# Masked graph attention on one core: two loads of W_v's blocks issued behind the opening products of the last q pair

## The chip, the cores and the metric

The kernel runs on one core of a Trainium2 chip, in float32. The metric is the device time of one execution in microseconds, as the median of repeated runs. Positions in the text, such as 366.93, are microseconds from the start of the span of the profiled execution.

## The reference

One layer of graph attention over 2708 nodes with 1024 features, with a sparse 0/1 matrix adj (about 0.15% ones, some four neighbours a node):

```python
h = relu(layernorm(x))
q = h @ W_q.T + b_q;  k = h @ W_k.T + b_k;  v = h @ W_v.T + b_v
z = (q @ k.T) / sqrt(1024) * adj
attn = softmax(where(z == 0, -10000, z), axis=1)
out = x + relu(attn @ v)
```

## The kernel before, in words

**What is computed instead.** The scores need q and k only where adj has a one, so the kernel doesn't form k: it builds M = W_q^T W_k / 32 at the start, computes q = h M (for all rows but the last 148), and takes the dot product of a row of q with the gathered rows of h of its neighbours. The weighted sum is taken over rows of h too (u = attn h), and W_v is applied last: o = u W_v. Rows are sorted by their number of neighbours, so that a tile of 128 rows needs few gathers.

**Stages on TensorE.** First the products that make M (up to about 104 us), then ten *q pairs* (`q_pairs`, two tiles of 128 rows each, units 0 to 9), then ten *o pairs* (`o_pairs`, units 10 to 19) and a lone tile. Every unit is a 256 x 1024 by 1024 x 1024 product in Strassen's form with seven products: `multiply` (L1046) and, for the first two, `opened` (L1015). The operands from the rows are a11, a12, a22 and s1 to s4; the weights are the blocks of M (M[:, 0, 0] and so on) and four differences T[:, 0] to T[:, 3], which live in the buffer that traces call wlow. One product is four matmuls of 128x512 in the source and eight in the trace (two passes each). The two opening products of unit n+1 (a11 by M[:, 0, 0] and s1 by T[:, 0], or by M[:, 0, 1] in an o unit) are issued inside unit n by `between` (L1031), ahead of unit n's last product, a22 by T[:, 3].

**The change of weights.** Between the last q pair (unit 9, `last_q`, tiles 18 and 19) and the first o pair M has to turn into W_v while both are in use. W_v's four blocks are loaded by `of_wv`: B22 into T[:, 0] (from where ACT copies it to M[:, 1, 1] and DVE subtracts to form T[:, 1]), B11 into M[:, 0, 0], B21 into M[:, 1, 0]; B12 less B11 is formed earlier in M[:, 0, 1]. The function `after(i)` (L1249) is called between the products of a unit; the loads of B22 and B11 are issued at `after(0)` of unit 9, B21 at `after(3)`. The place T[:, 0] is free when the second opening product of unit 9 has read it, the place M[:, 0, 0] when the first has.

**Queues.** Loads and stores of plain shape are issued by SP (its hardware queue is q1 in the profile), some stores by ACT (q10), and gathers by POOL (the software queue q0). SP and POOL issue in program order, and an instruction that waits holds up all behind it. The results of a q pair are stored to q_late by `store` inside `q_results` (L1086): tile ta after its right half, tile tb after ACT has copied the left half (`c21`, L1101). POOL fetches a tile's q back as `pq` (L833) when its scores are due; for tile 17 that is soon after its store.

**DVE** runs in an order written out by hand (`manual_schedule`): its share of gathered rows (L863 for the scores, L923 for the sums) is cut into pieces by `advance` and put between the additions of the products. One of those, L1093 (`c22`), reads the PSUM bank Y (psy) and makes the right half of the second tile; in the last q pairs it reads Y directly, so the product a22 by T[:, 3], which adds onto the same bank, must come after it:

```python
    def c22(Y, p5):
        behind.append(nc.vector.tensor_add(qb[:, hi], copied(Y) if EARLY <= ta < EARLY + 4 else Y, p5))
```

Of the kernel before, what the change touches and what calls it, by code (L numbers as in the profile page):

```python
# [65 lines left out]
def tile_preln_masked_attention(  # L66
# [12 lines left out]
    nc = tc.nc  # L79
# [120 lines left out]
    M = core.tile([P, 2, 2, 4, NB], FT, name="M")  # L200
# [108 lines left out]
    def follow(steps):  # L309

        for step in steps.split():
            first, *only = step[1:].split(".")
            first, *last = first.split("-")
            first = int(first or 0)
            if step[0] == "s":
                stats(range(first, int(last[0] if last else first) + 1))
            elif step[0] == "m":
                moments(first)
            elif step[0] == "r":
                root(first)  # L320
            elif step[0] == "a":
                apply(first, *[range(int(o[0]), int(o[-1]) + 1) for o in only])
            elif step[0] in "hk":
                keep(first, step[0] == "h")
            elif step[0] == "+":
                owe(first)
            elif step[0] == "p":
                counted(first)
            elif step[0] == "c":
                counts(*halves[first])  # L330
            elif step[0] == "o":
                sorted_at.append(sort(*halves[first]))
            elif step[0] == "w":
                pooled.close()
                with tc.issue_after((behind if first < EARLY else products)[-1].ins):
                    entered.append(put(first, int(last[0]) + 1))
            elif step == "z":
                pooled.enter_context(tc.manual_schedule(engines={mybir.EngineType.Pool}))
                with tc.issue_after(entered[-1].ins):
                    reload(EARLY, NT)  # L340
            elif step[0] == "b":
                reload(*halves[first])
            elif step[0] == "g":
                squared(first)
            else:
                if step[0] == "e":
                    counted(first)
                if step[0] != "j":
                    found(first, *[range(int(o[0]), int(o[-1]) + 1) for o in only])
                if step[0] != "i":  # L350
                    listed(first)
# [81 lines left out]
    T = wlow.rearrange("p (k a) (b w) -> p k (a b) w", a=2, b=2)  # L433
# [12 lines left out]
    with tc.tile_pool(name="w", bufs=1, side="left") as wp:  # L446
# [11 lines left out]
        t1 = [work.tile([P, D], FT, tag="hT", name=f"t1_{k}", bufs=2) for k in range(2)]  # L458
# [145 lines left out]
    def small(name):  # L604
        return half.tile([P, NB], FT, tag="half", name=name, bufs=14)
# [402 lines left out]
    def add_block(bank, a, b, last=True):  # L1008
        for c in range(4):
            mm = nc.tensor.matmul(bank, a[:, c, :], b[:, c, :], start=False, stop=(c == 3), skip_group_check=True)  # L1010
        return mm
# [3 lines left out]
    def opened(n):  # L1015

        if n not in banks_of:
            return
        X, Z = banks_of[n]
        ops = ops_of[n][0]  # L1020
        add_block(X, ops["a11"], M[:, 0, 0])
        Y = psum.tile([P, NB], FT, tag="acc", name="psy")
        nc.scalar.copy(Y, X)
        if n == FIRST:
            follow("o0")
        products.append(add_block(Z, ops["s1"], T[:, 0] if units[n][0] == "q" else M[:, 0, 1]))
        p5 = small("p5")
        nc.scalar.copy(p5, Z)
        opened_of[n] = Y, p5

    def between(n):  # L1031

        if n == len(units) - 1:
            single["first"] = one_started(single["banks"], single["turned"][:, 0:4, :])
        else:
            opened(n + 1)

    def one_started(banks, a):

        X, Z = banks  # L1040
        add_block(X, a, M[:, 0, 0])
        first = small("p_single")
        nc.scalar.copy(first, X)
        return first

    def multiply(n, results, after):  # L1046


        X, Z = banks_of.pop(n)
        ops = ops_of.pop(n)[0]  # L1050
        Y, p5 = opened_of.pop(n)
        after(0)
        after(1)
        products.append(add_block(Y, ops["s2"], T[:, 1]))
        u2 = small("u2")
        nc.scalar.copy(u2, Y)
        after(2)
        add_block(X, ops["a12"], M[:, 1, 0])
        results[0](X)
        after(3)  # L1060
        products.append(add_block(Z, ops["s4"], M[:, 1, 1]))
        results[2](Z, u2)
        after(4)
        products.append(add_block(Y, ops["s3"], T[:, 2]))
        results[1](Y, p5)
        after(5)
        between(n)
        add_block(Y, ops["a22"], T[:, 3])
        results[3](Y)
        after(6)  # L1070
# [119 lines left out]
    def of_wv(i, j):  # L1190

        return wv[j][:, i * 4:(i + 1) * 4, :]
# [26 lines left out]
    last_q = len(q_pairs) - 1  # L1219
# [13 lines left out]
    for n, unit in enumerate(units):  # L1233
# [15 lines left out]
        def after(i):  # L1249
# [15 lines left out]
                    with tc.issue_after(sorted_at[-1].ins):  # L1265
                        nc.vector.memset(g, 0.0)
            b11, t1, b21, b22 = M[:, 0, 0], M[:, 0, 1], M[:, 1, 0], M[:, 1, 1]
            for at, place, src in (((-2, 0), t1, of_wv(0, 0)), ((0, 0), T[:, 0], of_wv(1, 1)), ((0, 0), b11, of_wv(0, 0)),
                                   ((0, 3), b21, of_wv(1, 0))):
                if (n - last_q, i) == at:  # L1270
                    nc.sync.dma_start(place, src)
            if (n - last_q, i) == (0, 4):
# [302 lines left out]
```

## Time and profile before

| | |
|---|---|
| median of 3 runs | 630.65 us (630.48 to 630.88) |
| the profiled execution | 635.63 us |
| its span | 633.9 us |
| mean granted TensorE clock | 0.994 |
| HBM read, written | 146.70 MB, 43.36 MB |

The profile is one execution, taken by the hardware profiler. PE is TensorE's matmuls and PEld its weight loads, DVE VectorE, ACT ScalarE, POOL GpSimd, SP the sync engine; SPq or POOLq is an engine's sequencer or queue. A row such as `ps<-M,a` names what an instruction writes and reads, without the buffers' numbers; a bracket at a row's end tells how long the engine stood idle before it and what ended that. The granted clock is a share of TensorE's full clock. A tile has 128 x 1024 float32 values, 0.52 MB; a block of W_v is 128 x 2048, 1.05 MB.

### The profile page before, as it was taken

The page shows a single profiled execution, that of the slowest core. Times are in us where ns is not written, and L with a number is a line of the kernel's source. Part 1 is how long each engine was busy: PE and PEld are TensorE (multiplying, and loading weights), DVE is VectorE, ACT ScalarE, POOL GpSimd, SP SyncE. Part 2 cuts the span into 40 slices and gives each one's busy share as a digit, 9 for nine tenths or more (in the row PEclk, how much of TensorE's full clock was granted, in tenths as well). Part 3 has the DMA queues.
Part 4 walks back from the last instruction along what each step waited for, and adds up shares of the span by engine and source line. Part 5 has one row for each costly group of instructions (what it writes and reads, how often), then busy time and mean ns, then how long its engine had stood idle before and what let it go on. Part 6 is the DMA issues. An engine that isn't in the chain of part 4 may idle for free.

```text
span 633.9 us, 6066 instructions
## 1 busy us (share of the span) xinstructions
PE 623.0 (98%) x1579; PEld 312.0 (49%) x1579; DVE 525.2 (83%) x1022; ACT 291.6 (46%) x421; POOL 370.7 (58%) x394
## 2 busy tenths in 40 slices
PE   9999999999998999999999989999999999999996
PEld 5777766444444544444444434444444444444442
DVE  5999879898897845899897879998988998988741
ACT  3538985749477372443332333444433324342300
POOL 2639960885766677666543432878566776762241
PEclk9999999999999999999999989999999999999999
DMA  8999997598788469996686999899999999996391
GB/s 333 407 365 316 340 351 301 207 320 307 262 257 337 135 196 369 296 410 191 207 343 197 362 346 305 261 335 318 330 285 344 291 297 307 341 286 172 102 295 71
DMA packets 65089, 182.19 MB, mean 287 GB/s; under 512 B 9960, under 2 KB 20024, under 8 KB 64409
## 3 DMA queue, kind: packets, MB, share of 16 engines
q0 software_dynamic: 26656, 86.02, 43.3%
q1 hardware_dynamic: 31594, 71.53, 32.7%
q10 hardware_dynamic: 6798, 24.20, 9.8%
q8 instruction: 14, 0.23, 0.2%
q14 instruction: 27, 0.21, 0.1%
HBM read 146.70 MB, written 43.36 MB: 300 GB/s over the span
## 4 chain that ended last, share of the span: by engine, by line
PE 96%; DMA 3%; issue 0%; POOL 0%; SPq 0%; DVE 0%; ACT 0%; POOLq 0%
PE ps L1010 44%; PE psy L1010 32%; PE ps_y L476 6%; PE ps_x L476 4%; PE ps_z L476 4%; PE pt L415 3%; DMA M<-in_wv_dram 2%; DMA qr<-h_dram,tab 1%; PE ps_y L511 1%; PE ps_h L1226 0%; PE ps_v L594 0%; DVE y_alone L1391 0%; POOL out_dram L1375 0%; ACT q L1101 0%; POOLq L1397 0%
## 5 line engine op out<-in xcount | busy, mean ns | idle before, releaser
L610 POOL DMA_INDIRECT g<-h_dram,tab x93 | 120.5, 1296 | 62.7 <-ACT u L912 21.7
L1010 PE MATMUL ps<-M,a 128*128 128x512 f32 x320 | 145.8, 599 | 2.0 <-DMA M<-in_wv_dram 2.0
L1010 PE MATMUL psy<-wlow,s 128*128 128x512 f32 x320 | 145.1, 596 | 0.0
L863 DVE SCALAR_TENSOR_TENSOR junk<-g,pq 128x1024 uint8<-128x1024 f32 x92 | 112.4, 1221 | 11.8 <-issue 4.9
L1010 PE MATMUL ps<-M,s 128*128 128x512 f32 x240 | 107.9, 592 | 0.0
L1010 PEld LDWEIGHTS ps<-M,a 128*128 128x128 f32 x320 | 60.4, 192 | 75.4 <-issue 71.2
L1010 PEld LDWEIGHTS psy<-wlow,s 128*128 128x128 f32 x320 | 60.6, 192 | 72.9 <-issue 71.9
L923 DVE SCALAR_TENSOR_TENSOR u<-g,coef,u 128x1024 f32<-128x1024 f32 x70 | 89.7, 1281 | 5.5 <-ACT u L912 4.0
L389 DVE FIND_INDEX8 at<-ones,adj 128x8 uint32<-128x685 f32 (+1 forms) x88 | 74.5, 865 | 0.0
L1010 PEld LDWEIGHTS ps<-M,s 128*128 128x128 f32 x240 | 45.5, 190 | 57.2 <-issue 56.5
L1010 PE MATMUL psy<-wlow,a 128*128 128x512 f32 x160 | 71.9, 592 | 0.0
L368 ACT ACTIVATE sized<-adj 128x2708 uint8<-128x2708 f32 (+1 forms) x22 | 54.2, 2465 | 7.9 <-DMA adj<-in_adj_dram 6.6
L1111 POOL DMA_INDIRECT y<-in_x_dram,tab x19 | 34.6, 1821 | 35.6 <-ACT y L1128 24.2
L298 POOL TENSOR_TENSOR hsum<-hsum,x 128x256 f32<-128x256 f32 (+1 forms) x56 | 38.8, 738 | 25.5 <-DVE wlow L444 21.4
L1010 PEld LDWEIGHTS psy<-wlow,a 128*128 128x128 f32 x160 | 30.4, 190 | 38.3 <-issue 37.1
L808 POOL DMA_INDIRECT out_dram<-y,tab x21 | 27.0, 1287 | 19.2 <-issue 13.1
L1010 PE MATMUL ps<-wlow,s 128*128 128x512 f32 x80 | 36.0, 593 | 0.0
L944 ACT COPY v<-u 128x1024 f32<-128x1024 f32 x19 | 19.8, 1044 | 29.1 <-DVE u L923 25.8
L760 ACT COPY ps<-bp_sb 128x512 f32<-128x512 f32 x42 | 24.6, 595 | 10.3 <-DVE y L1146 9.7
L626 POOL DMA_INDIRECT tab_dram<-tab,pos_i x22 | 21.7, 985 | 11.2 <-DVE pos_i L689 5.7
L276 ACT ACTIVATE x<-x,r 128x1024 f32<-128x1024 f32 (+1 forms) x22 | 25.8, 1232 | 5.2 <-POOL r L266 5.2
L912 ACT ACTIVATE u<-g,coef 128x1024 f32<-128x1024 f32 x16 | 18.4, 1149 | 21.3 <-DVE coef L911 13.2
(253 smaller groups left out, 843.4 us busy)
## 6 DMA issues: line engine op xcount, KB each, us to landing
adj<-in_adj_dram SPq DMA_DIRECT2D x21, 1354.0 KB
x<-in_x_dram SPq DMA_DIRECT2D x21, 512.0 KB
h_dram<-x ACTq DMA_DIRECT2D x21, 512.0 KB
u_dram<-v ACTq DMA_DIRECT2D x19, 512.0 KB
or<-u_dram SPq DMA_DIRECT2D x76, 128.0 KB
q_late<-q SPq DMA_DIRECT2D x12, 512.0 KB
pq<-q_late POOLq DMA_DIRECT2D x12, 512.0 KB
M<-in_wv_dram SPq DMA_DIRECT2D x3, 1024.0 KB
```

Of the source, the lines that this page charges most:

```text
L276: nc.scalar.activation(xs[i][:n], xs[i][:n], AF.Relu, bias=r[:n, 4, i:i + 1], scale=r[:n, 3, i:i + 1])
L298: small.append(nc.gpsimd.tensor_add(hsum[:n, cols], hsum[:n, cols], xt[:n, cols]))
L368: nc.scalar.activation(sized[:n], a[:n, :, :PW], AF.Abs, accum_out=total[:n, t:t + 1])
L389: nc.vector.max_index(at[:n, k - first_k, g, :], ones[:n, 0:8], a[:n, g, :])
L476: mm = nc.tensor.matmul(bank, a_tile(o + H * a[0], a[1], i), b(o), start=first and o == 0, stop=(o == H - 1), skip_group_check=True)
L610: return nc.gpsimd.indirect_dma_start(out=dst, out_offset=None, in_=src, in_offset=off, bounds_check=N - 1, oob_is_err=False)
L760: nc.scalar.copy(return_[h], row[:, h * NB:(h + 1) * NB])
L808: to = nc.gpsimd.indirect_dma_start(out=out, out_offset=bass.IndirectOffsetOnAxis(ap=ptab.bitcast(U32)[:n, t, SLOTS:SLOTS + 1], axis=0), i ...
L863: chained(lambda: nc.vector.scalar_tensor_tensor(junk, g_of[t][s], 1.0, tq[t], op0=ALU.mult, op1=ALU.mult, accum_out=zall[:, t, s:s + 1]))
L923: chained(lambda: nc.vector.scalar_tensor_tensor(u, g_of[t][s], coef[:, s:s + 1], u, op0=ALU.mult, op1=ALU.add))
L1010: mm = nc.tensor.matmul(bank, a[:, c, :], b[:, c, :], start=False, stop=(c == 3), skip_group_check=True)
L1111: return nc.gpsimd.indirect_dma_start(out=y[:n], out_offset=None, in_=x, in_offset=off, compute_op=ALU.add)
```

## The change

The two loads leave `after(0)` of unit 9 and are issued in `between`, at the point where unit 8 has issued the opening products of unit 9:

```diff
         else:
             opened(n + 1)
+        if n == last_q - 1:
+            nc.sync.dma_start(T[:, 0], of_wv(1, 1))
+            nc.sync.dma_start(M[:, 0, 0], of_wv(0, 0))
...
-            for at, place, src in (((-2, 0), t1, of_wv(0, 0)), ((0, 0), T[:, 0], of_wv(1, 1)), ((0, 0), b11, of_wv(0, 0)),
-                                   ((0, 3), b21, of_wv(1, 0))):
+            for at, place, src in (((-2, 0), t1, of_wv(0, 0)), ((0, 3), b21, of_wv(1, 0))):
```

Lines below the addition are three numbers higher in the changed kernel as far as the loop of loads, and two behind it (L1086 is L1089, L1093 is L1096, L1271 is L1273).

On SP's queue, around the end of unit 8, before (or_5 and or_4 are rows for the first two o pairs; q_17 is the second result of unit 8; wlow is T[:, 0]):

```order
L700 DMA or_5_2263<-u_dram_66 32x4x256 [waits DMAHW6_49]
L700 DMA or_5_2263<-u_dram_66 32x4x256 [waits DMAHW7_49]
L1086 DMA q_late_65<-q_17_2153 128x1024 [waits DMAHW0_49,DVE_49,Activation_49]
L1271 DMA wlow_170<-in_wv_dram 128x2048 [waits DMAHW2_49,PE_49]
L1271 DMA M_147<-in_wv_dram 128x2048 [waits DMAHW3_49]
L1271 DMA M_147<-in_wv_dram 128x2048 [waits DMAHW4_49,PE_49]
L700 DMA or_4_2370<-u_dram_66 32x4x256 [waits DMAHW5_49,DMASW2_49,Pool_49]
```

and of the change:

```order
L700 DMA or_5_2263<-u_dram_66 32x4x256 [waits DMAHW6_49]
L700 DMA or_5_2263<-u_dram_66 32x4x256 [waits DMAHW7_49]
L1038 DMA wlow_170<-in_wv_dram 128x2048 [waits DMAHW0_49,PE_49]
L1039 DMA M_147<-in_wv_dram 128x2048 [waits DMAHW2_49]
L1089 DMA q_late_65<-q_17_2153 128x1024 [waits DMAHW3_49,DVE_49,Activation_49]
L1273 DMA M_147<-in_wv_dram 128x2048 [waits DMAHW4_49,PE_49]
L700 DMA or_4_2370<-u_dram_66 32x4x256 [waits DMAHW5_49,DMASW2_49,Pool_49]
```

The store of tile 17's q, which waits for ACT and DVE, has moved from ahead of the two loads to behind them; the names DMAHW0 to DMAHW7 are semaphores that transfers take in turn. Nothing else changes places, on any engine.

On POOL's queue, at the fetch of tile 17's q, before (g are gathered rows, the last of six in a row shown; pq_17 and pq_13 are fetched tiles of q):

```order
L610 DMA g1_1426<-h_dram_63,tab_97 128x1024 [waits DMASW6_49,DVE_49]
L610 DMA g3_1428<-h_dram_63,tab_97 128x1024 [waits DMASW7_49,DVE_49]
L833 DMA pq_17_2353<-q_late_65 128x1024 [waits DMAHW0_49,DMASW0_49]
L833 DMA pq_13_2434<-q_late_65 128x1024 [waits DMASW1_49,DVE_49]
L610 DMA wlow_170<-h_dram_63,tab_97 128x1024 [waits DMASW2_49,DMAHW2_49,DVE_49,Activation_49]
```

and of the change:

```order
L610 DMA g1_1426<-h_dram_63,tab_97 128x1024 [waits DMASW6_49,DVE_49]
L610 DMA g3_1428<-h_dram_63,tab_97 128x1024 [waits DMASW7_49,DVE_49]
L833 DMA pq_17_2353<-q_late_65 128x1024 [waits DMAHW3_49,DMASW0_49]
L833 DMA pq_13_2434<-q_late_65 128x1024 [waits DMAHW0_49,DMASW1_49,DVE_49]
L610 DMA wlow_170<-h_dram_63,tab_97 128x1024 [waits DMASW2_49,DMAHW0_49,DVE_49,Activation_49]
```

The rows stand in the same order; the fetch of pq_17 waits for the store of tile 17 under that store's new semaphore.

DVE's rows behind the subtraction that forms T[:, 1], of the change (u_20 is a sum, q_18 and q_19 are the halves of unit 9's results, junk2 and zall take scores of tile 17):

```order
L1284 TENSOR_TENSOR wlow_170<-wlow_170,M_147 128x2048 [waits DMAHW0_49,PE_49]
L923 SCALAR_TENSOR_TENSOR u_20_2321<-g2_1427,coef_2320,u_20_2321 128x1024 [waits DMASW4_49,Activation_49]
L1099 TENSOR_TENSOR q_18_2299<-ps1_2224,u2_2317 128x512 [waits PE_49]
L863 SCALAR_TENSOR_TENSOR junk2_2390,zall_102<-g6_1431,pq_17_2353 128x1024 [waits DMASW0_49]
L863 SCALAR_TENSOR_TENSOR junk2_2392,zall_102<-g7_1432,pq_17_2353 128x1024 [waits DMASW1_49,DVE_49]
L1096 TENSOR_TENSOR q_19_2300<-psy_2280,p5_2286 128x512 [waits PE_49]
```

Before, these six stand in the same order, as L1282, L923, L1096, L863, L863 and L1093; the subtraction waits for DMAHW2 there. Behind the opening products of unit 10 PE's product that adds onto the bank psy_2280 waits for the last of them, before and now.

## The prediction

> **What bounds the kernel now.** I read the page's busy shares first, then who waited for whom on PE, then the chain that ended last, then the timelines of PE, DVE and POOL around the one wait that the change touches. The page, and the two long waits of PE:
>
> ```profile
> PE 623.0 (98%) x1579; PEld 312.0 (49%) x1579; DVE 525.2 (83%) x1022; ACT 291.6 (46%) x421; POOL 370.7 (58%) x394
> PE pt L415 <- DMA qr<-h_dram,tab: 2.1, 1, 2.1
> PE ps L1010 <- DMA M<-in_wv_dram: 2.0, 1, 2.0
> ```
>
> PE is busy 98% of the span, and it waits for data twice. The second wait is for a block of W_v in M, that is B11, needed by the opening product of the first o unit. The chain that ended last, in order of time, shows what made B11 late (start us, us, what):
>
> ```profile
> 351.20 0.59 ACT q L1101
> ...
> 351.81 0.34 SPq L1086
> ...
> 352.25 0.38 SPq L1271
> ...
> 352.95 13.84 DMA M<-in_wv_dram
> ```
>
> SP first waits for ACT to finish tile 17's q (L1101), issues its store (L1086), then the two loads. B11 is issued at 352.95 and takes 13.84 us. The price on PE, from its timeline (start, duration, form, count):
>
> ```profile
> 344.13 3.60 PE L1010 MATMUL ps<-wlow,s 128*128 128x512 f32 x8
> ...
> 361.30 3.60 PE L1010 MATMUL psy<-wlow,s 128*128 128x512 f32 x8
> 366.93 5.37 PE L1010 MATMUL ps<-M,a 128*128 128x512 f32 x8 [2.03 <-DMA M<-in_wv_dram]
> 372.13 3.60 PE L1010 MATMUL ps<-M,s 128*128 128x512 f32 x8
> 375.57 3.60 PE L1010 MATMUL psy<-wlow,a 128*128 128x512 f32 x8
> ```
>
> Products start 3.43 us apart when nothing is late (375.57 - 372.13 is 3.44). The opening product could have started at 361.30 + 3.43 = 364.73 and started at 366.93: 2.20 us. It then took 372.13 - 366.93 = 5.20 us instead of 3.43: another 1.77 us. The second part is the clock. Stretches of the span: columns are PE, PEld, DVE, ACT and POOL busy us, then PE's granted clock, DMA share and GB/s:
>
> ```profile
> 196.00:206.00 10.00, 7.92 (x22) 3.94 (x21) 6.46 (x23) 6.06 (x10) 8.11 (x11) 0.87 0.82 302
> 367.00:372.00 5.00, 5.00 (x8) 2.11 (x9) 2.05 (x3) 0.00 (x0) 3.37 (x3) 0.66 1.03 355
> ```
>
> Right behind the wait the clock was 0.66 over 5 us, that is 1.7 us lost; behind the other wait (2.08 us idle between 196 and 206) it was low as well. So a wait of some 2 us costs nearly 4: 2.20 + 1.77 = 3.97 us is all that the change can take away directly.
>
> **The change: what it removes.** T's B22 place is last read by the product that starts at 344.13 and ends about 347.6; the B11 place is free still earlier. SP has nothing else queued then, so B22 is issued at about 347.7 instead of 352.25 and B11 at 348.4 instead of 352.95, 4.5 us sooner. B11 could take up to 16 us and still be there for 364.73; it took 13.84. Both old waits on these loads (PE's 2.20 + 1.77, and below DVE's 1.71) go. Instruction counts and the order on PE, DVE, ACT and POOL stay as they were, so no work is added.
>
> **What is late next.** Two products behind that opening product PE depends on DVE: the product psy<-wlow,a at 375.57 (a22 times T3 of the last q pair) adds onto the bank Y that DVE has to read first, in the addition that makes tile 19's right half (L1093). DVE's timeline there, then POOL's:
>
> ```profile
> 364.17 2.29 DVE L1282 TENSOR_TENSOR wlow<-wlow,M 128x2048 f32<-128x2048 f32 x1 [1.71 <-DMA wlow<-in_wv_dram]
> ...
> 371.21 1.23 DVE L863 SCALAR_TENSOR_TENSOR junk<-g,pq 128x1024 uint8<-128x1024 f32 x1 [2.95 <-DMA pq<-q_late]
> ...
> 373.63 0.69 DVE L1093 TENSOR_TENSOR q<-psy,p 128x512 f32<-128x512 f32 x1
> ```
>
> ```profile
> 353.99 1.74 POOL L610 DMA_INDIRECT g<-h_dram,tab  x1 [0.53 <-DVE u L929]
> 359.75 1.15 POOL L833 DMA_DIRECT2D pq<-q_late  x2 [4.02 <-DMA q_late<-q]
> ```
>
> DVE stood 2.95 us at 371.21 until tile 17's q (pq) was back on chip, and L1093 is third in line behind that. It ends at 373.63 + 0.69 = 374.32. Today PE comes at 375.57 and notices nothing. With the old wait gone PE comes at 364.73 + 2 x 3.43 = 371.59 and has to wait till about 374.35, if pq lands when it lands now: 2.75 us.
>
> So what counts is by how much pq moves; call it d (negative is sooner). DVE's earlier 1.71 us don't help: they only lengthen its wait for pq. Pq is fetched by POOL, behind its gathers on the software queue q0, and only after the store of tile 17, which stands on SP's queue q1. The DMA queues in 350-356, 356-364 and 364-371 (packets, MB, share of the engines):
>
> ```profile
> DMA packets 461, 1.69 MB, mean 281 GB/s; under 512 B 49, under 2 KB 49, under 8 KB 461
> q0 software_dynamic: 435, 1.58, 82.1%
> ...
> DMA packets 747, 3.43 MB, mean 429 GB/s; under 512 B 86, under 2 KB 86, under 8 KB 571
> q1 hardware_dynamic: 310, 1.86, 55.4%
> q0 software_dynamic: 293, 1.04, 31.9%
> ...
> q1 hardware_dynamic: 365, 1.83, 63.8%
> q0 software_dynamic: 373, 0.88, 37.5%
> ```
>
> and from SP's timeline seven row loads of the next o unit but one:
>
> ```profile
> 358.49 12.76 SPq L700 DMA_DIRECT2D or<-u_dram  x7
> ```
>
> In 350-356 the gathers have the engines nearly alone, at 281 GB/s; once the W_v loads run, everything together moves at 429, but q0 falls from 1.58 MB in 6 us to 1.04 in 8. The moved loads bring this squeeze forward by some 5 us. Two bounds for d. Below: about 5.5 us at 429 instead of 281 GB/s move 0.8 MB more, which at 400 GB/s is 2.0 us; if all of it came to q0, d = -2.0. Above: the store now has both loads (128 x 2048 f32 each, 2.1 MB) ahead of it on q1. At q1's 1.83 MB in 7 us they take 8.0 us, less the 4.1 us by which they are issued sooner than the store is (347.7 against 351.81): the store lands up to 3.9 us later, POOL asks for pq that much later, and if nothing hides it, d = +3.9. What hides it: q0 moved 0.88 MB in 364-371, of which pq is 0.52, so 0.36 MB of older gathers stood ahead of pq even at 364. And the 0.8 MB gained at the front meets seven row loads of 0.13 MB each, 0.92 MB, that stand ready on q1 and take their turns against q0, where today they move mostly after pq. Both bounds are thus nearly used up, and I take **d = -0.2**.
>
> The sum: -3.97 (old wait and its slow clock) + 2.75 - 0.2 = 2.55 (new wait) + 1.77 (its slow clock, since two waits of 2.0 to 2.1 us both had it) = **+0.35 us**. [...]
>
> All this is made on the profiled execution, 635.63 us with a span of 633.9; it lies 0.8% above the median of 630.65. I carry the difference over to the median: 630.65 + 0.35 = **631.0 us**. A difference within 0.2%, 1.26 us, can't be told from none.
>
> **Rivals.**
> *Full gain.* If pq lands by 371.21 - 2.75 = 368.46, PE never waits: 630.65 - 3.97 = 626.7. For it: B11 is surely early, and the profiled execution may be more crowded than the timed ones. Against: d would have to pass its lower bound of -2.0; at that bound 0.75 us of wait remain, 627.4. The gain would last to the end, although the lone tile is tight there:
>
> ```profile
> 609.07 1.25 DVE L705 STREAM_TRANSPOSE T_alone<-or 128x1024 f32<-128x1024 f32 x1 [10.76 <-DMA or<-u_dram]
> 610.78 3.60 PE L1010 MATMUL ps<-M,T_alone 128*128 128x512 f32 x8
> DVE u L1127 <- PE ps L1010: 3.0, 4, 1.2
> DVE p L1123 <- ACT taken L1077: 2.9, 3, 1.6
> ```
>
> T_alone is ready at 610.32, 0.46 us ahead of PE; but DVE, whose sums feed it, waits 5.9 us for PE's results between 460 and 560 alone (the last two rows), so it moves up with PE by the 3.97.
>
> *The new wait without the slow clock.* The wait of 2.55 us is there, but the clock holds: -3.97 + 2.55 = -1.42, 629.2 us, just past the limit of what can be told. Two waits out of two that were slowed speak against it; for it, both of those ended with the clock's drop at once, so how far into a wait the drop is decided can't be read. [...]
>
> *Slower: the store behind the loads.* POOL's request for pq waits for a store that now queues behind both loads. If the gathers ahead of pq are through before it has landed, nothing hides the rest: with half of the 3.9 us showing, d = +2.0, the wait is 4.75 and the sum -3.97 + 4.75 + 1.77 = +2.55, 633.2 us; with all of it +4.45, 635.1. It decides from d = +0.7 (wait 3.46) on: then the time is over 1.26 us longer. For it: only 0.36 MB of gathers were left at 364, less than 2 us of work. Against: they are squeezed sooner now and so last longer.
>
> *No change in what is issued when.* Something else on SP holds the loads until 352: 630.65. The queue shows nothing between the last row load of the unit before and these loads, so this is unlikely.
>
> **How the numbers follow.** The forecast (wait moved, clock halved, d between -1.5 and +0.7) gets 0.52, full or nearly full gain 0.10, the wait without slow clock 0.16, slower 0.20, no change 0.02. With d in these bounds the sum is between -0.95 and +1.25, within the limit but for sizes that are off (0.03 on either side). Of the third case 0.09 is beyond the limit and 0.07 within. Faster: 0.10 + 0.09 + 0.03 = 0.22; slower: 0.20 + 0.03 = 0.23; the same: 0.46 + 0.07 + 0.02 = 0.55. The range goes from 627.4 (d = -2.0, which leaves most of the full gain out) to 633.2 (half of the store's delay showing): some 0.17 stay outside.
>
> **What would show it.** Right: B22 and B11 issued near 347.7 and 348.4; PE's wait for M gone; in its place a wait of 2 to 3 us of a psy product for DVE's q addition, near 371.6, with the clock below 1 behind it; pq at DVE within 1 us of 371.2. Wrong: no wait of PE there (full gain), the clock at 1.00 behind the wait, or a pq later than 371.9. The forecast as a whole fails if PE's products behind the last q pair start over 1.3 us sooner or later than now.

## The result, and the profile after

| | before | after |
|---|---|---|
| median of 6 runs each, side by side | 630.75 us (630.23 to 631.53) | 635.98 us (634.79 to 638.39) |
| ratio to before, 95% interval | | 1.0085 [1.0072, 1.0098] |
| the profiled execution | 635.63 us | 635.39 us |
| its span | 633.9 us | 633.6 us |
| mean granted clock of the profiled execution | 0.994 | 0.992 |

The change costs 5.2 us; the prediction was 631.0 with a range up to 633.2. The two profiled executions are equally long although the medians differ by 5.2 us: the one of before was unusually long for its kernel, 5 us over its median, and one place where that shows is a wait near 200 us (`pt`, 2.1 us, with the clock at 0.50 from 203.42 to 206.84) that the profile of after doesn't have. So positions are compared from one common mark, the start of the second opening product of unit 9 (`ps<-wlow,s`), at 344.13 before and 340.40 after; after's positions are 3.73 us lower by nothing that the change does.

The waits of PE, of after (us in total, times, longest):

```profile
PE psy L1010 <- DVE q L1096: 4.2, 1, 4.2
```

The wait for M, B11, isn't among them any more, and one for DVE's addition out of bank Y has come. SP's queue and PE's timeline, of after:

```profile
344.03 0.35 SPq L1038 DMA_DIRECT2D wlow<-in_wv_dram  x1
344.43 0.43 SPq L1039 DMA_DIRECT2D M<-in_wv_dram  x1
348.08 0.33 SPq L1089 DMA_DIRECT2D q_late<-q  x1
```

```profile
340.40 3.60 PE L1010 MATMUL ps<-wlow,s 128*128 128x512 f32 x8
...
361.00 3.60 PE L1010 MATMUL ps<-M,a 128*128 128x512 f32 x8
364.44 3.60 PE L1010 MATMUL ps<-M,s 128*128 128x512 f32 x8
372.28 6.37 PE L1010 MATMUL psy<-wlow,a 128*128 128x512 f32 x8 [4.25 <-DVE q L1096]
378.48 3.60 PE L1010 MATMUL psy<-wlow,s 128*128 128x512 f32 x8
```

The loads go out 4.5 us sooner than before, as foreseen (344.03 + 3.73 = 347.76). The opening product on B11 starts on time. The product behind the next, a22 by T[:, 3], was due at 364.44 + 3.43 = 367.87 and starts at 372.28: 4.41 us late. The one behind it follows 6.20 us later instead of 3.43, so the slow clock takes 2.77 us more. The chain that ended in this wait, and DVE's timeline:

```profile
347.47 0.59 ACT q L1104
...
348.08 10.76 DMA q_late<-q
...
359.39 0.49 POOL pq L833
...
359.93 10.29 DMA pq<-q_late
...
371.62 0.62 DVE q L1096
```

```profile
369.12 1.23 DVE L863 SCALAR_TENSOR_TENSOR junk<-g,pq 128x1024 uint8<-128x1024 f32 x1 [6.40 <-DMA pq<-q_late]
...
371.54 0.69 DVE L1096 TENSOR_TENSOR q<-psy,p 128x512 f32<-128x512 f32 x1
```

It is the chain that the prediction followed: store of tile 17, fetch, two scores, addition, PE. The row of 10.29 us begins at 359.93, with POOL's second fetch (tile 13's, issued right behind), and ends after DVE's first score of tile 17 has begun. Tile 17's own fetch was issued at 359.36 and landed 9.7 us later; that is what DVE waited for. Pq reaches DVE 369.12 - 340.40 = 28.72 us after the mark, before it was 371.21 - 344.13 = 27.08: the shift d is +1.64 us where -0.2 was taken.

Where d comes from stands in the DMA queues. The prediction's stretches 350-356, 356-364 and 364-371 of before are 346.27-352.27, 352.27-360.27 and 360.27-367.27 of after:

```profile
DMA packets 412, 2.36 MB, mean 394 GB/s; under 512 B 36, under 2 KB 36, under 8 KB 211
...
q1 hardware_dynamic: 217, 1.65, 69.6%
q0 software_dynamic: 195, 0.72, 32.1%
...
DMA packets 712, 3.06 MB, mean 382 GB/s; under 512 B 81, under 2 KB 81, under 8 KB 597
...
q0 software_dynamic: 293, 1.07, 35.6%
...
q0 software_dynamic: 539, 1.45, 66.6%
q1 hardware_dynamic: 532, 0.87, 37.4%
```

The first stretch moves 0.67 MB more than before (2.36 against 1.69), and all of that and more goes to q1: q0, the gathers, fall from 1.58 to 0.72 MB. In the second q0 stays level (1.07 against 1.04), in the third it makes up 0.57 MB (1.45 against 0.88). It is 0.26 MB short where pq should land, at 1.45 MB in 7 us some 1.3 us of work. The third stretch moves 2.33 MB in all against 2.70 before: what the engines gained at the front they lose again at the end, when q1 has less to add (0.87 MB against 1.83). This is the account of one execution; the runs below show that the bytes on q0 alone don't set how late pq is.

### The profile page after: what moved, and what is told of

The parts are those of the page before. It is cut to its first block, busy times and chain, and to the rows that moved or that the text cites. A ratio compares the mean times of both kernels' runs of the same rounds, so it can differ in the third digit from the quotient of the medians.

```text
span 633.6 us, 6066 instructions
## 1 busy us (share of the span) xinstructions
PE 622.3 (98%) x1579; PEld 311.6 (49%) x1579; DVE 524.4 (83%) x1022; ACT 291.5 (46%) x421; POOL 367.0 (58%) x394
## 4 chain that ended last, share of the span: by engine, by line
PE 90%; DMA 5%; DVE 2%; ACT 1%; issue 0%; POOL 0%; POOLq 0%; DVEq 0%; ACTq 0%
PE ps L1010 41%; PE psy L1010 30%; PE ps_y L476 7%; PE ps_x L476 4%; PE ps_z L476 4%; PE pt L415 3%; DMA adj<-in_adj_dram 2%; DMA q_late<-q 2%; DMA pq<-q_late 2%; DVE at L389 1%; PE ps_y L511 1%; PE ps_h L1229 0%; PE ps_v L594 0%; ACT sized L368 0%; DVE junk L863 0%
## 5 line engine op out<-in xcount | busy, mean ns | idle before, releaser
L1010 PE MATMUL ps<-M,a 128*128 128x512 f32 x320 | 144.0, 592 | 0.0
L863 DVE SCALAR_TENSOR_TENSOR junk<-g,pq 128x1024 uint8<-128x1024 f32 x92 | 112.4, 1221 | 14.0 <-DMA pq<-q_late 6.4
L923 DVE SCALAR_TENSOR_TENSOR u<-g,coef,u 128x1024 f32<-128x1024 f32 x70 | 89.7, 1281 | 5.5 <-ACT u L912 4.1
L1010 PE MATMUL psy<-wlow,a 128*128 128x512 f32 x160 | 74.7, 611 | 4.2 <-DVE q L1096 4.2
L476 PE MATMUL ps_y<-wlow 128*128 128x512 f32 x64 | 27.6, 592 | 0.0
```

The lines of the kernel that those rows point to most:

```text
L476: mm = nc.tensor.matmul(bank, a_tile(o + H * a[0], a[1], i), b(o), start=first and o == 0, stop=(o == H - 1), skip_group_check=True)
L863: chained(lambda: nc.vector.scalar_tensor_tensor(junk, g_of[t][s], 1.0, tq[t], op0=ALU.mult, op1=ALU.mult, accum_out=zall[:, t, s:s + 1]))
L923: chained(lambda: nc.vector.scalar_tensor_tensor(u, g_of[t][s], coef[:, s:s + 1], u, op0=ALU.mult, op1=ALU.add))
```

## The experiments

The first four runs were made to tell two theories apart. A: the store of tile 17 waits on q1 behind the two loads, and pq with it. B: the loads take the engines from everything, the gathers on q0 as well as the store. Ratios are to runs of before on the same chip.

### Which queue, which block, or when

**The store on ACT's queue.** The change, with the store of tile 17 issued by ACT (q10, which also carries ACT's stores of u) instead of SP:

```diff
-            (nc.scalar if t < 4 else nc.sync).dma_start(dst, q)
+            (nc.scalar if t < 4 or t == 17 else nc.sync).dma_start(dst, q)
```

> The change, with the store of tile 17's q issued by ACT (queue q10) instead of SP, so that it no longer stands behind the two loads. Theory A (the store behind the loads makes pq late, DVE's addition late, and PE wait at the bank Y): the store lands by 357 instead of 358.8 in that trace's time, pq is then held only by the gathers ahead of it, d falls from +1.6 to between -0.5 and 0, PE's wait for DVE from 4.2 to 2.2-2.7 us with one slow window: 630.5 to 632.5 us, at least 3 us under the change. Theory B (the squeeze: both loads take the engines from the gathers ahead of pq, wherever the store stands): pq is as late as in the change, 635 to 636.5 us.

Measured: 636.56 us against 631.3, ratio 1.0081 [1.0068, 1.0094]. The chain of this kernel:

```profile
347.50 9.91 DMA q_late<-q
...
357.94 11.77 DMA pq<-q_late
```

On a queue with no load ahead the store still takes 9.91 us (10.76 in the change), and pq comes 29.91 us after the mark (369.73 - 339.82), later than in the change. Theory A fell: what stands ahead on SP's queue isn't the point. That the store is late at all still counts for something, since POOL asks for pq only when it has landed.

**Only B11 early.** B22 goes back to its old place (the loop of loads, not shown, has it again):

```diff
         if n == last_q - 1:
-            nc.sync.dma_start(T[:, 0], of_wv(1, 1))
             nc.sync.dma_start(M[:, 0, 0], of_wv(0, 0))
...
```

> Half of the change: B11 issued behind the opening products, B22 left behind the store at its old place. The store has one load ahead of it instead of two. Theory A: the store is about half as late, d between 0 and +0.8, PE's wait for DVE 2.7 to 3.5 us with one slow window: 631 to 633 us, between the two kernels. Theory B: the squeeze starts as early as in the change but with half the bytes: also between, so this run tells A from B only by where the store lands against pq. If B22's later arrival (it is needed for T1 and by ACT for M) costs on its own, it is above 636.

Measured: 631.41 us, ratio 1.0001 [0.9987, 1.0015]. PE's and DVE's rows:

```profile
370.65 5.40 PE L1010 MATMUL psy<-wlow,a 128*128 128x512 f32 x8 [2.87 <-DVE q L1095]
```

```profile
367.49 1.23 DVE L863 SCALAR_TENSOR_TENSOR junk<-g,pq 128x1024 uint8<-128x1024 f32 x1 [3.24 <-DMA pq<-q_late]
```

Here pq comes 27.34 us after the mark (340.15), d = +0.26, and the forecast's picture is what one sees: the wait for B11 is exchanged for one of 2.87 us for bank Y, and the time is the same.

**Only B22 early.** The load of B11 goes back instead.

> Only the load of B22 is issued early, ahead of the store of tile 17; B11 stays behind it. Theory B (the two early loads together squeeze the gathers and the store of tile 17, so pq comes late and PE waits for the addition that reads bank Y): one load ahead of the store squeezes half as long, pq at DVE +0.3 to +1.2 us against before, B11 about as late as before (wait 1.5 to 2.5 us), time 630 to 633. Rival C (it is B22's load, which runs in the gathers' stretch, that does the whole harm, since B11 alone did none): 634 to 637, pq at DVE +1.5 us or later.

Measured: 638.86 us against 634.13, ratio 1.0079 [1.0057, 1.0101], all of the harm with one of the two loads. PE's row there:

```profile
375.60 6.77 PE L1010 MATMUL psy<-wlow,a 128*128 128x512 f32 x8 [3.88 <-DVE q L1095]
```

Theory B had expected less and missed; rival C, that it is B22's load, fitted the time, though pq came 28.35 us after the mark (d = +1.27), a little less late than it had said. The store is nearly on time here (7.97 us); the fetch takes 12.16 us, and PE's wait for B11 is gone here too (its load is issued 8.07 us after the mark, in before 8.82). But B22 also starts later than B11 alone did: it must wait for the second opening product, 3.63 us after the mark (347.72 - 344.09), while B11 alone was issued 0.19 us after it (340.34 - 340.15). So the block and the time had to be parted.

**B11 alone, held back.** A load of 64 KB that waits as B22 does stands ahead of it (shown against B11 alone):

```diff
         if n == last_q - 1:
+            nc.sync.dma_start(T[:, 0, 0, 0:128], of_wv(1, 1)[:, 0, 0:128])
             nc.sync.dma_start(M[:, 0, 0], of_wv(0, 0))
...
```

> Only B11 is issued early, but held back on SP's queue behind a load of 64 KB into a corner of T[:, 0], which must wait until the second opening product has read that place: B11 then starts some 3.5 us later than in the run with B11 alone, where B22 starts in the run with B22 alone, about 4 us ahead of the store. Theory B' (the harm comes from the time at which 1 MB of weights meets the gathers and the store, whichever block it is): the store lands late, pq at DVE +0.8 to +1.8 us, PE waits 3.5 us or more for the addition that reads bank Y, ratio to before 1.005 to 1.010, as with B22 alone (1.0079). Rival C (B22's load or what hangs on it does the harm): ratio 0.998 to 1.003, as with B11 alone (1.0001).

Measured: 635.99 us against 630.95, ratio 1.0067 [1.0047, 1.0088]. In the profiled execution B11 was issued 1.45 us after the mark, not 3.6 (its wait was shorter, as only the corner had to be free), and even that sufficed. The profile was of an execution of 632.75 us, with pq only 0.43 us late; so the kernel was profiled again:

> The kernel with B11 alone, held back, once more for a second profile: the first was of an execution of 632.75 us, while the median of ten was 635.99. Theory B': in an execution near 636 pq is at DVE +0.8 to +2.0 us late and PE waits 3.5 us or more, with one or two windows at half clock behind it. If an execution near 636 has pq no later than +0.5 and PE's wait at 3 us, the loss lies somewhere else and B' doesn't explain the time.

That execution took 640.78 us, longer than any of the ten before (637.19 at most), and PE waited 5.93 us. Its chain:

```profile
351.50 7.58 DMA q_late<-q
...
359.60 14.60 DMA pq<-q_late
```

Rival C fell: issued 1.26 us later, B11's load does nearly the harm of B22's. And this chain has a store of usual length; pq is 3.32 us late (374.22 - 343.82 = 30.40) though POOL asked for it when it always had (15.78 us after the mark, 15.81 in the first profile). It is the fetch that took longer, 14.60 us against 11.68 in the first profile.

What the slower kernels have in common is that q0 moved less in the first 12 us after the mark, when POOL issues the gathers. Of before, of B11 alone, of B11 held back (first and second profile), of B22 alone, and of the change:

```profile
q0 software_dynamic: 862, 2.78, 75.1%
```

```profile
q0 software_dynamic: 857, 2.77, 65.8%
```

```profile
q0 software_dynamic: 759, 2.41, 61.8%
...
q0 software_dynamic: 768, 2.45, 63.5%
```

```profile
q0 software_dynamic: 691, 2.18, 56.7%
```

```profile
q0 software_dynamic: 614, 1.88, 47.9%
```

B11 issued at +0.19 (340.34) goes out ahead of all but the first of the eight gathers that POOL issues from 340.1 to 350.0; q1 moves 1.35 MB in the 12 us instead of 0.38, and q0 loses nothing (2.77 MB): ratio 1.0001. With 0.33 to 0.90 MB lost the ratios are 1.0067, 1.0079 and 1.0085. That orders the kernels, not their executions: with B11 held back q0 lost as much in the first profile as in the second, and pq was 0.43 us late in the one and 3.32 in the other. What makes the difference between these two isn't shown.

### The link through pq and bank Y

**Bank Y copied by ACT**, so that PE needn't wait for DVE's addition, in the change and in before:

```diff
-... copied(Y) if EARLY <= ta < EARLY + 4 else Y, p5))
+... copied(Y) if EARLY <= ta < EARLY + 4 or ta == BARE - 2 else Y, p5))
```

> The change, with the bank Y of the last q pair copied out by ACT (0.59 us) ahead of DVE's addition, as the earlier pairs 8 to 11 do, so that PE's product a22 x T3 waits for ACT and not for DVE. If the bank Y is the only link from the late pq to PE (A and B alike): PE's wait of 4.2 us and its slow clock go, and the whole gain forecast for the direct effect shows: 626 to 628 us. If there is a second link close behind (the subtractions that form T2 and T3, or the rows of the second o pair): PE waits there, 629 to 633.

> The kernel before with the same ACT copy of Y: a control. In the profile of before DVE's addition was over 1.26 us ahead of PE, so the copy frees nothing: 630.2 to 631.3 us. If the timed executions of before wait there too, or if the copy alone is worth something, it is faster than 630.

Measured: 633.36 us, 1.0027 [1.0016, 1.0038], and 629.99 us, 0.9978 [0.9969, 0.9987]. The first is slower than expected even with a second link; in the control the copy is worth something by itself. In the change the copy takes away the wait for bank Y with its slow clock, but not the whole loss: its PE waits further on.

```profile
PE psy L1010 <- ACT u L1059: 1.7, 1, 1.7
PE ps L1010 <- DVE T_alone L705: 1.6, 1, 1.6
```

DVE stood 7.83 us for pq in this kernel. That its lateness is what arrives at these two waits, the second of them at the lone tile that the prediction had called tight, is likely but not shown. With B11 alone early DVE is less late:

> Only B11 is issued early, and ACT copies bank Y for the last q pair, so that PE need not wait for DVE there. B11 alone moved pq by only +0.3 us and moved PE's wait from B11 to bank Y (2.87 us with a slow clock after it). If that exchange is all that kept the early B11 from paying, PE waits at neither place: 2.0 to 4.0 us less than before, 626.8 to 629.0. If the DVE and ACT chain behind it is what bounds (the second link seen in the copy with both loads early), PE waits for the formed operands of the next unit instead and the time is that of the copy alone, 629.5 to 631.

Measured: 632.39 us against 634.13 (one of the twelve runs, 640.21, left out), 0.9972 [0.9952, 0.9992]; that is the copy's own gain in before (0.9978) within the intervals, and less than hoped. The profile shows 1.5 us of waiting for T_alone and 1.4 us for ACT's psy instead. DVE stood only 3.48 us for pq here, so waits of this kind come without the long one too.

**Tiles 17 and 13 in the other order**, so that the two scores ahead of the addition need a q that was stored long before:

```diff
-    order = [6, 5, 4, 3, 2, 0, 20, 7, 17, 13, 18, ...
+    order = [6, 5, 4, 3, 2, 0, 20, 7, 13, 17, 18, ...
```

> The change, with tiles 17 and 13 of one o pair taken in the other order: the scores that stand ahead of the addition reading bank Y need tile 13's q, which was stored long before, and tile 17's is needed later. Theory B with the chain store, fetch, scores, addition, PE: DVE no longer stands before that addition, PE's wait for it goes (from 4.2 to under 1 us), and the time falls by 4 to 8 us against the change, to 627 to 632. Rival (PE is late because DVE itself has too much work there, or the gathers and not tile 17's q hold the scores): the wait stays at 3 us or more, 634 to 637.

> Control for the swapped tiles: before, with tiles 17 and 13 in the other order. DVE's wait of 2.95 us for tile 17's q goes, but PE's wait for B11 (2.0 us) stays, so theory B expects the time of before, 629.5 to 632. If the order of the tiles matters by itself (other numbers of gathered rows, gathers earlier or later), it is off by over 1.3 us and the swapped change has to be read against this run.

Measured: 631.95 us, 0.9955 [0.9937, 0.9973] with the change, and 633.43 us, 0.9988 [0.9969, 1.0008] without it (before: 634.13). PE of the first:

```profile
367.94 3.60 PE L1010 MATMUL ps<-M,s 128*128 128x512 f32 x8
371.38 3.60 PE L1010 MATMUL psy<-wlow,a 128*128 128x512 f32 x8
374.81 3.60 PE L1010 MATMUL psy<-wlow,s 128*128 128x512 f32 x8
```

No product is late. The squeeze is as large as in the change, with 1.85 MB on q0 in the first 12 us; it no longer costs anything, since nobody needs tile 17's q that soon. This is the run that shows the link: the order of two tiles turns the change from 1.0085 to 0.9955. The control didn't go quite as expected: its time is that of before, but in its profile PE's wait for B11 is 0.7 us instead of 2.0, so the other order helps that load a little as well. With B11 alone and the swap:

> B11 alone early, and tiles 17 and 13 in the other order: neither of the two waits of the change, and the least squeeze on the store. If what is left of PE's waits decides, the time is that of the change with the swapped tiles (ratio 0.9955) within 0.002: 0.993 to 0.998. If the early B22 still cost something there, it is below 0.994.

Measured: 627.83 us against 630.95, 0.9956 [0.9942, 0.997]. It and the change with the swap are the versions that compute the layer and beat before by most, about 2.8 us; the copy in before and the copy with B11 alone gain 1.4 and 1.8 us.

**Old rows for tile 17's q**, so that its fetch needn't wait for the store (the kernel leaves out tile 17's own q: its scores are then those of tile 13's rows):

```diff
+            at = 13 if t == 17 else t
-            nc.gpsimd.dma_start(tq[t], q_late[(t - EARLY) * P:(t - EARLY + 1) * P, :])
+            nc.gpsimd.dma_start(tq[t], q_late[(at - EARLY) * P:(at - EARLY + 1) * P, :])
```

> The change, but the fetch of tile 17's q reads the rows of tile 13 in q_late, stored long before (tile 17's scores are then of other rows; nothing else is left out). POOL need not wait for the store. If the store is what makes pq late, POOL asks 3 us or more sooner, pq is at DVE by 369 (d -2 or less), PE's wait for bank Y falls below 1.5 us and the ratio to before is 0.992 to 0.997. Rival (the backlog of gathers on q0 holds pq, and the store hides behind it): pq at DVE within 1 us of where the change has it, PE waits 3 us or more, ratio 1.005 to 1.010.

Measured: 627.84 us, 0.9957 [0.9944, 0.997], no wait of PE. It doesn't part the store from the gathers, as it was meant to: freed of the store, the fetch also moved ahead of the gathers in POOL's order (issued at 335.36 against 359.36). It says the same as the swap: with pq there, the change gains 2.7 us.

**The fetch on SP's queue**, where it passes the gathers but still waits for the store, in the change and in before:

```diff
-            nc.gpsimd.dma_start(tq[t], q_late[(t - EARLY) * P:(t - EARLY + 1) * P, :])
+            (nc.sync if t == 17 else nc.gpsimd).dma_start(tq[t], q_late[(t - EARLY) * P:(t - EARLY + 1) * P, :])
```

> The change, with the fetch of tile 17's q issued by SP (q1, behind the load of B21 and ahead of the row loads) instead of POOL (q0, behind the gathers); it still waits for the store. If pq is late because it stands behind the squeezed gathers on q0, it now passes them: at DVE 1 us or more sooner than before the change (d of -1 or less), PE's wait for bank Y under 2 us, ratio to before 0.992 to 1.000. If it is late because the store lands late behind the two loads, the fetch is asked for as late as in the change and pq comes at d of +1 or later, PE waits 3.5 us or more, ratio 1.005 to 1.010.

> Control: before, with the same fetch issued by SP. PE's wait for B11 (2.0 us) stays; pq comes sooner than by POOL (d of -1 or less) if the gathers on q0 are what it waits behind, and DVE's 2.95 us of waiting shrink, without a gain for PE: ratio 0.996 to 1.002. If the row loads that now stand behind the fetch come too late for the first o pairs, it is above 1.002.

Measured: 637.13 us, 1.0048 [1.0024, 1.0073], and 635.02 us, 1.0033 [1.0012, 1.0053], against 633.97. DVE's first score, of the change and of the control:

```profile
371.63 1.23 DVE L863 SCALAR_TENSOR_TENSOR junk<-g,pq 128x1024 uint8<-128x1024 f32 x1 [5.42 <-DMA pq<-q_late]
```

```profile
371.01 1.23 DVE L863 SCALAR_TENSOR_TENSOR junk<-g,pq 128x1024 uint8<-128x1024 f32 x1 [5.46 <-DMA pq<-q_late]
```

Neither expectation came true. Pq comes 27.74 us after the mark in the change (371.63 - 343.89), 1.0 us sooner than by POOL, and 29.26 us in the control (371.01 - 341.75), 2.2 us later than by POOL: asked for at +15.0 there, it took 14.2 us on q1 behind the loads. In the first profile of before the engines were full in this stretch (a share of 1.03 from 356 to 364 and of 1.01 from 364 to 371), and the fetch came late behind the loads (29.26 us in the control) as behind the gathers (28.72 in the change).

### How certain the slow clock is

**Before and after once more**, for a second profile of each.

> The kernel before once more, for a second profiled execution. If the slow clock behind the wait for B11 is certain, the wait is 1.7 to 2.3 us and the product behind it takes 5.2 us again. If it depends on where the wait falls in the clock's windows, the product can take 3.5 to 3.7 us behind the same wait, and then the first profile overstated what the change could take away by 1.77 us.

> The change once more, for a second profile. If the first is typical, PE waits 4 to 5 us for the addition that reads bank Y, pq is at DVE +1.0 to +2.5 us and the clock is at half for one or two windows of 3.4 us; the execution takes 634.5 to 638.5 us. If the wait is below 3 us in an execution of that length, the time went elsewhere.

Before took 630.37 us this time, and PE's timeline reads:

```profile
357.06 3.60 PE L1010 MATMUL psy<-wlow,s 128*128 128x512 f32 x8
362.66 3.67 PE L1010 MATMUL ps<-M,a 128*128 128x512 f32 x8 [2.01 <-DMA M<-in_wv_dram]
366.17 3.60 PE L1010 MATMUL ps<-M,s 128*128 128x512 f32 x8
370.25 3.70 PE L1010 MATMUL psy<-wlow,a 128*128 128x512 f32 x8 [0.48 <-DVE q L1093]
373.79 3.60 PE L1010 MATMUL psy<-wlow,s 128*128 128x512 f32 x8
```

The same wait of 2.0 us, and the next product follows after 3.51 us: no slow clock. The 15 runs of before beside it have mean clocks of 0.997 to 1.000, eleven of them 0.998 or more. A single stretch of 3.41 us at half clock takes 1.71 of some 630 us and leaves 0.997 at most, so those eleven had none. The profiled execution of the prediction, with two such windows, has 0.994, and six of the 25 runs of before beside the first four experiments are as low (0.994 or 0.995). The six runs of after have 0.992 to 0.996. After, on a chip where before took 633.1 us, took 638.79, with PE's wait at 6.63 us. That is longer than expected, in the same place, with pq 31.10 us after the mark (d = +4.02), and here the store was the late one (13.38 us, then 9.49 for pq).

## Why the prediction was wrong

**The place, the chain and the exchange of waits were right.** B22 and B11 were issued within 0.3 us of where they were expected, the wait for B11 went, and the wait for L1096 came at the product named, with a slow clock behind it. B11 alone, issued at +0.19, is the forecast come true in its size too (2.87 us, no change of the time).

**The step that failed: "Both bounds are thus nearly used up, and I take d = -0.2".** Measured in the profile d is +1.64, and with it the wait is 4.41 instead of 2.55 us, just what the prediction's own 2.75 + d gives. The lower bound rested on the 0.8 MB that the engines would move more at the front; they did (0.67 MB in the first stretch), but q0 got none of it and lost 0.86 MB. The sum over all queues was taken for that of the queue on which pq stands. The prediction's own row, q0 at 1.58 MB alone and 1.04 MB beside q1, said what q0 loses when q1 has work. The reserve that the upper bound was set against was misread too. The 0.88 MB of 364-371 aren't one pq and 0.36 MB of older gathers: tile 13's fetch stands right behind, the two make 1.05 MB, and between 364.1 and 366.1 q0 moved 0.03 MB, so the gathers were all but through by then. The gathers lost their share when loads stood beside them: in the first stretch 82.1% of the engines went to q0 before, 32.1% after.

**The part of the store was half right.** It lands late, 10.76 us after its issue (7.08 in the second profile of before); 3.7 us more is close to the upper bound's 3.9. Tile 17's fetch is then shorter, 9.7 us against 11.9 in that profile of before, so part of the delay is hidden, as the prediction said, but less of it than d = -0.2 needs: POOL asks 18.96 us after the mark instead of 15.62, 3.34 us later, and pq comes 1.64 us later. In the second profile of after POOL asks 5.97 us later and pq comes 4.02 later, and with the store on ACT's queue 2.50 and 2.83. Since the store is late on ACT's queue as well, the working of the upper bound by the order on q1 doesn't hold, whatever its size. The rival *Slower: the store behind the loads* gave the right time, 633.2 to 635.1 with the limit at d = +0.7, by a mechanism that is only part of the matter. How much of d is the store's and how much is the fetch's behind the gathers stays open: two executions had the store on time and only the fetch slow (B22 alone, and B11 held back in its second profile), another mostly the store, and the fetch on SP's queue gained 1.0 us and told no more.

**The second step that failed: the clock, mis-sized twice.** Taken from one execution, the slow clock behind the old wait (1.77 of the 3.97 us) was counted as a gain, but the second profile of before does without it, and by their mean clocks so do most of its timed runs. Behind the new wait it cost 2.77 us instead of 1.77, since two windows were slow. The balance, by the second profile of before: the old wait 362.66 - 357.06 - 3.43 = 2.17, clock 0.08; new wait 4.41, clock 2.77; the change costs 4.41 + 2.77 - 2.17 - 0.08 = +4.9 us. Against the forecast's +0.35 that is 4.6 us more, of which the later pq makes 1.9 and the two sizes of the clock 1.7 and 1.0: the clock is the greater part of the miss. Before also lost 0.65 + 0.11 us at bank Y in that execution, which makes the cost +4.2. With the second profile of after, over the same stretch from the mark, it is +5.4 (382.02 - 342.69 against 373.79 - 339.89). The medians say +5.2, between the two; single executions of after differ by more than that gap (634.79 to 638.39).

**The other rivals.** Full gain came only where the link was cut (0.9955 to 0.9957, about 2.8 us instead of 3.97, since the slow clock mostly wasn't there to be won; the second profile of before has 2.17 + 0.08 + 0.65 + 0.11 = 3.0 us at the two waits). *The new wait without the slow clock* did not come: behind each of the seven waits of over 3.0 us (3.04 to 6.63) the clock was at half, with 5.02 to 6.61 us from that product to the next instead of 3.43. Behind shorter ones it varies: 2.87 us with B11 alone had it (5.23 us to the next product), 3.00 us in the control with the fetch on SP's queue did not (3.54).

## What to carry to other kernels

A load that is moved forward into a stretch where another queue has the DMA engines nearly to itself took bytes from that queue here (1.58 to 0.72 MB) while the total rose: price it by what that queue loses there, and by who waits for the last transfer on it, not by the total that moves. Before a wait is removed, look for the next one on the same engine with less slack than the wait is long; here two tiles in another order made that slack and turned a loss of 0.85% into a gain of 0.45%. Take the price of a wait from several executions where the clock is part of it.

## What the runs showed of the hardware

In the first profile of before and in that of after, the last stage left aside, the clock was at half for 3.41 us or twice that, and these stretches do not start with the wait. In before it is 0.50 from 203.42 to 206.84 and from 367.26 to 370.68; the two begin 163.84 us apart, which is 48 such lengths, and the second begins 0.33 us after PE's wait has ended (366.93). In after it is 0.50 from 370.86 to 377.69, beginning 1.42 us ahead of the wait's end (372.28). A length of 3.41 us counted from such a change is called a window here. In the stretches below, each a window, the columns are PE, PEld, DVE, ACT and POOL busy, then PE's clock, DMA share and GB/s. Of before (first profile), of before (second profile), of the store on ACT's queue, and of after:

```profile
363.85:367.26 3.41, 1.38 (x4) 0.49 (x3) 3.09 (x2) 1.99 (x2) 0.03 (x1) 1.00 1.02 422
367.26:370.68 3.42, 3.42 (x5) 1.35 (x4) 1.00 (x2) 0.00 (x0) 2.81 (x3) 0.50 1.01 365
```

```profile
358.92:362.33 3.41, 1.73 (x5) 0.42 (x3) 2.73 (x2) 1.99 (x2) 0.00 (x0) 1.00 1.03 422
362.33:365.75 3.42, 3.09 (x8) 1.44 (x9) 1.35 (x2) 0.00 (x0) 2.49 (x3) 1.00 1.01 376
```

```profile
365.95:369.36 3.41, 1.50 (x4) 0.38 (x2) 0.00 (x0) 0.00 (x0) 0.00 (x0) 1.00 1.05 314
369.36:372.77 3.41, 0.00 (x0) 0.00 (x0) 3.00 (x6) 0.00 (x0) 0.00 (x0) 1.00 1.02 384
372.77:376.19 3.42, 3.30 (x4) 1.51 (x5) 2.75 (x13) 2.21 (x5) 0.00 (x0) 0.50 1.06 332
```

```profile
367.45:370.86 3.41, 0.58 (x2) 0.00 (x0) 1.70 (x3) 0.00 (x0) 0.00 (x0) 1.00 1.03 323
370.86:374.27 3.41, 1.99 (x3) 0.96 (x4) 2.81 (x13) 1.47 (x4) 0.00 (x0) 0.50 1.05 328
374.27:377.69 3.42, 3.42 (x6) 1.36 (x5) 3.32 (x4) 1.48 (x3) 0.93 (x1) 0.50 1.03 349
```

A window in which PE was busy 1.38 us is followed by one at half clock, one with 1.73 or 1.50 us is not. In the second profile of before the clock doesn't change in this stretch, so where its windows begin isn't shown; divided as above, the same wait of 2.0 us that falls into one window in the first profile is split over two in the second. After's second window has 1.99 us busy, but at half clock, and another slow one follows. In the 17 windows read around such waits in seven profiles, with busy time at half clock counted half, each with 1.40 us of work or less was followed by a slow one (1.40 us, 2.80 at half clock, with B22 alone), and none with 1.50 us or more (1.50 us with the store on ACT's queue). That is an observation and was not tested by itself. In the first profile of before 2.03 us without work in one window (3.41 - 1.38) were enough. A slow window costs 1.7 us of PE's work (half of 3.41), so a wait's price jumps: the same 2 us cost 2 or nearly 4, and the change's 4.41 us over 7, with two windows.

What else the runs show is how much one execution differs from the next at the same place: in the change the store took 10.76 us in one profile and 13.38 in another, and with B11 held back the fetch took 11.68 and 14.60 us.
